# Moving two blocks of GpSimd sums at the start of a fused attention, MLP and adapter kernel

## The chip, the cores and the metric

One NeuronCore of a Trainium2 chip runs the whole program. The metric is the device time of one execution in microseconds (us), as the median of several runs. All data is float32. The engines are TensorE (PE; its weight loads are shown apart, as PEld), VectorE (DVE), ScalarE (ACT), GpSimd (POOL) and SyncE (SP). SP, ACT and POOL each also issue DMAs from their own queue; an engine works through its queue in order, and an instruction that waits holds up all behind it.

## The reference

Four sequences of 512 tokens of width 512 go through two layers. Shortened to what matters:

```python
# layer 0
q, k, v = x @ Wq, x @ Wk, x @ Wv
attn = softmax(q @ k.T * V ** -0.5)
attn_out = (attn @ v) @ Wp + bp
cms_out = gelu(attn_out @ cW1 + cb1) @ cW2 + cb2 + one_hot(target_codes)
concat = concatenate([attn_out, cms_out])
modifier = gelu(concat @ mW1 + mb1) @ mW2 + mb2
x = clip(x + cms_out + modifier, 0, 1)
# layer 1: one of three adapters for each sequence, chosen by stream
h = x + gelu(x @ W_down[stream] + b_down[stream]) @ W_up[stream] + b_up[stream]
out = layernorm(h) * ln_w[stream] + ln_b[stream]
```

## The kernel before

Every large product is made with seven block products in place of eight (Winograd's form of Strassen's scheme), in the MLP layers at two levels. A product of a left operand with blocks a11, a12, a21, a22 and a right operand with blocks b11, b12, b21, b22 needs four sums of the left blocks (s1 to s4) and four of the right (t1 to t4) besides the blocks themselves; the seven products are numbered 1 to 7, and product 5 takes s1 and t1, 6 takes s2 and t2, 7 takes s3 and t3, 3 takes s4, and 4 takes t4. `seven` runs them in a given order and combines them in PSUM with VectorE; when a block of the result is complete it calls `keep(half, columns, ps)`.

Two weights are folded ahead of their use: Wq with Wk to w_qk (cms0), and Wv with Wp to w_vp (cms1). `folded` does this with `small_product`, which takes the products in the order 1, 2, 5, 6, 7, 3, 4. The blocks of the result are complete after product 2 (half 0, columns 0), 7 (1, 1), 3 (0, 1) and 4 (1, 0), and `keep` copies each to w with ScalarE and has VectorE make the four sums of w, since w is next used as a left operand.

The four sequences go in two pairs. For each pair the loop in the kernel's body forms u = w_qk with x (`pair_product`, L638), then for each of the two sequences a softmax (`softmax`, whose matmuls are in `small_product` at L704), then the product of x's rows with the turned softmax (`small_product` again, left operand `left_operand(x_rows[s0 + k], s_x[k])`), and last w_vp with the two results. The sums of x's rows, s_x, are made by GpSimd in `left_sums`, which calls `weight_sums` (L198 to L201: s1, s2, s3, s4; s3 does not depend on s1). In pair 0 those of sequence 0 go to wslot2 and those of sequence 1 to wslot0, which before holds the sums of u that the first softmax uses. wslot2 also holds the sums of Wp that `right_sums` makes for the fold of w_vp (L741), so that the sums of sequence 0 are written, and made, behind that fold.

GpSimd also prepares the weights of the later layers. This is the generator `expansion`, of which `steps(expanding, n)` runs n parts. Its first part issues the loads of the raw cW1 blocks (`load_c1`, four DMAs, L235) and of x for sequences 2 and 3 (L142). `expand_c1` then has three parts for each of two units: four sums of 128x256 and a store from the upper half of slot1; eight sums of 128x512 into slot1, part and first, with the loads of the next raw blocks and two stores (c_outer, L258 and L259); and four sums of 128x256 with a store. Part and first are written again by the second unit, so that its sums wait for the stores of the first unit to land. Behind it come cW2 and mW1 (`expand`, L362 and L365).

x's first two sequences, Wv and Wp are loaded from SP's queue at the start, in this order, Wp into slot3; the sequences' rows stay in the tiles hidden.

The order of instructions within a queue is not that of the text. The framework under the kernel tracks the dependences of tiles and plans each engine's queue by its own costs: of the instructions that it takes for ready it places the one first that was written first. `keep_in_program_order` pins single instructions. So a move in the text shifts priorities, and the place in the queue is a result.

The part of the pair loop that the change touches reads before it:

```python
if pair == 0:
    s_v, t_wp = sums_in(slot[2]), sums_in(wslot[2])
    right_sums(wp, t_wp)
    then[7] = [lambda: transposed(chunks(wv), wv_t, left_from_psum(wv_t, s_v))]
pair_product(lhs_qk, begun, u, beside=beside_u(s_u, u), then=then)
if pair == 0:
    lhs_vp = folded(left_operand(wv_t, s_v), right_operand(wp, t_wp), w_vp, s_v)
steps(expanding, 6)
if pair == 0:
    left_sums(x_rows[s0], s_x[0])
```

Of the kernel before, what the change touches and what calls it, by code (L numbers as in the profile page):

```python
# [18 lines left out]
def kernel(  # L19
# [38 lines left out]
    nc = tc.nc  # L58
# [36 lines left out]
    slot = [wide[:, 4 * i : 4 * i + 4, :].rearrange("p c n -> p (c n)") for i in range(2)]  # L95
    slot += [const.tile([P, 2048], F32, name=f"slot{i}") for i in range(2, 8)]
    wslot = [const.tile([P, 2048], F32, name=f"wslot{i}") for i in range(4)]
# [16 lines left out]
    def weight(engines, src, dst):  # L114

        w = dst.rearrange("p (c n) -> p c n", c=4)
        n = 4 // len(engines)
        rows = src.rearrange("(h c p) n -> h p c n", c=n, p=P)
        for i, eng in enumerate(engines):
            eng.dma_start(out=w[:, n * i : n * (i + 1), :], in_=rows[i])  # L120
        return w
# [19 lines left out]
    def load_x(b, eng, dst):  # L141
        eng.dma_start(out=dst, in_=x[b].rearrange("(t p) v -> p t v", p=P))  # L142
        return dst
# [5 lines left out]
    x_rows = [load_x(b, nc.sync, x_places[b]) for b in range(2)]  # L149
    wv = weight((nc.sync, nc.sync), Wv, slot[2])  # L150
    wp = weight((nc.sync, nc.sync), Wp, slot[3])
# [44 lines left out]
    def weight_sums(a11, a12, a21, a22, s1, s2, s3, s4, eng=None):  # L196
        eng = eng or nc.gpsimd
        eng.tensor_tensor(s1, a21, a22, ALU.add)  # L198
        eng.tensor_tensor(s2, s1, a11, ALU.subtract)
        eng.tensor_tensor(s3, a11, a21, ALU.subtract)  # L200
        eng.tensor_tensor(s4, a12, s2, ALU.subtract)  # L201
# [13 lines left out]
    def flat(t):  # L215
        return t.rearrange("p c n -> p (c n)")
# [204 lines left out]
    def expansion():  # L421

        c2_units = [(cW2, False, c2_kept, u) for u in range(2)]
        load_c1(0)

        for b in range(2, B):
            x_rows.append(load_x(b, nc.gpsimd, x_places[b]))
        yield from expand_c1(0, lambda: load_c1(1))
        yield from expand_c1(1, lambda: load_raw(cW2, False, 0, slot[4:6]))

        constants()
        yield from expand_all(
            c2_units + m1_units, slot[4:6], (flat(part), slot[3], slot[1]), flat(first)
        )
# [39 lines left out]
    def steps(gen, n):  # L474
        for _ in range(n):
            next(gen, None)

    expanding = expansion()


    def transposed(get, dst, finish=None):

        begin_transposed(get, dst, finish)()
# [19 lines left out]
    def chunks(t):  # L503
        return lambda c: t[:, c, :]
# [6 lines left out]
    w_qk, w_vp = cms  # L511
# [35 lines left out]
    def add(dst, a, b):  # L547
        nc.vector.tensor_tensor(dst, a, b, ALU.add)  # L548
# [9 lines left out]
    def minus(out_, one, two):  # L558
        nc.vector.tensor_tensor(out_, one, two, ALU.subtract)
# [99 lines left out]
    def halves(t):  # L659

        return t[:, 0:2, :256], t[:, 2:4, :256], t[:, 0:2, 256:], t[:, 2:4, 256:]

    def left_operand(t, s):

        a11, a12, a21, a22 = halves(t)
        s1, s2, s3, s4 = (s[:, k] for k in range(4))
        return {1: a11, 2: a12, 3: s4, 4: a22, 5: s1, 6: s2, 7: s3}

    def left_sums(t, s):
        weight_sums(*halves(t), *(s[:, k] for k in range(4)))  # L670

    def right_operand(t, s):

        b11, b21, b12, b22 = halves(t)
        t1, t2, t3, t4 = (s[:, k] for k in range(4))
        return {1: b11, 2: b21, 3: b22, 4: t4, 5: t1, 6: t2, 7: t3}
# [41 lines left out]
    def sums_in(t):  # L718
        return t.rearrange("p (k c n) -> p k c n", k=4, c=2)
# [14 lines left out]

        return finish

    def right_sums(t, s):
        b11, b21, b12, b22 = halves(t)
        t1, t2, t3, t4 = (s[:, k] for k in range(4))
        for out_, one, two in ((t1, b12, b11), (t2, b22, t1), (t3, b22, b12), (t4, b21, t2)):  # L740
            nc.gpsimd.tensor_tensor(out_, one, two, ALU.subtract)  # L741

    def folded(lhs, rhs, w, s, then=None):


        s1, s2, s3, s4 = (s[:, k] for k in range(4))
        held = []

        def keep(half, columns, ps):
            dst = w[:, 2 * half : 2 * half + 2, 256 * columns : 256 * columns + 256]  # L750
            nc.scalar.copy(dst, ps)
            if (half, columns) == (1, 1):
                held.append(ps)
            elif (half, columns) == (0, 1):
                minus(s3, w[:, 0:2, :256], ps)
                minus(s2, held[0], s3)
                add(s1, held[0], w[:, 0:2, 256:])
            elif (half, columns) == (1, 0):
                minus(s4, ps, s2)

        small_product(lhs, rhs, keep, then, order=(1, 2, 5, 6, 7, 3, 4))
        return left_operand(w, s)
# [63 lines left out]
    lhs_vp = None  # L826
    next_operands = None

    def places(pair):

        return big[2 + 2 * pair : 4 + 2 * pair], (big[6:8], big[0:2])[pair]

    def first_operand(pair):
        xT, t_x = places(pair)
        return begin_transposed(
            chunks(x_rows[2 * pair]), xT[0], right_from_psum(xT[0], sums_in(flat(t_x[0])))
        )
# [68 lines left out]
    for pair in range(B // 2):  # L906
        s0, s1 = 2 * pair, 2 * pair + 1
        xT, t_x = places(pair)
        t_x = [sums_in(flat(t)) for t in t_x]
        u = big[4 - 2 * pair : 6 - 2 * pair]  # L910
        attn = big[6:8]
        s_u = [sums_in(wslot[k]) for k in range(2)]
        s_x = [sums_in(wslot[k]) for k in (2, 0)]
        t_p = t_x
        then = {}
        wv_t = mod[0]
        if pair:
            left_sums(x_rows[s0], s_x[0])
            s_x[1] = sums_in(flat(attn[1]))
            left_sums(x_rows[s1], s_x[1])  # L920
        if pair == 0:

            s_v, t_wp = sums_in(slot[2]), sums_in(wslot[2])
            right_sums(wp, t_wp)
            then[7] = [lambda: transposed(chunks(wv), wv_t, left_from_psum(wv_t, s_v))]
        pair_product(lhs_qk, begun, u, beside=beside_u(s_u, u), then=then)
        if pair == 0:

            lhs_vp = folded(left_operand(wv_t, s_v), right_operand(wp, t_wp), w_vp, s_v)
        steps(expanding, 6)  # L930
        if pair == 0:
            left_sums(x_rows[s0], s_x[0])
        pT, mix = u, xT

        def turn(k):
            transposed(lambda t: mod[k][:, t, :], pT[k], right_from_psum(pT[k], t_p[k]))

        for k in range(2):
            softmax(
                k, left_operand(u[k], s_u[k]), right_operand(xT[k], t_x[k]),  # L940
                {7: [lambda: turn(0)]} if k else None,
            )
            if k == 0 and pair == 0:
                left_sums(x_rows[s1], s_x[1])
        for k in range(2):
            if k == 0:
                def keep(half, tokens, ps):
                    nc.scalar.copy(
                        mix[0][:, 2 * half : 2 * half + 2, 256 * tokens : 256 * tokens + 256], ps
                    )  # L950
            else:
                operands, take = second_operand(*mix, mod)
                held = []

                def keep(half, tokens, ps):

                    if (half, tokens) == (1, 1):
                        held.append(ps)
                        return
                    take(half, (slice(0, 2), slice(256 * tokens, 256 * tokens + 256)), ps)  # L960
                    if (half, tokens) == (0, 1):
                        take(1, (slice(0, 2), slice(256, 512)), held[0])

            small_product(
                left_operand(x_rows[s0 + k], s_x[k]), right_operand(pT[k], t_p[k]), keep,
                {7: [lambda: turn(1)]} if k == 0 else None,
                nc.scalar.copy if k else nc.vector.tensor_copy,
            )
            steps(expanding, 6)
        then = {}  # L970
        if pair == 0:
            begun = {}
            then = {6: [lambda: first_operand(1)()], 4: [lambda: begun.update(both_operands(1))]}

        pair_product(lhs_vp, operands, attn, bp_c, then=then, at=pT[0] if pair else None)
        for k in range(2):
            nc.scalar.dma_start(out=attn_kept[s0 + k], in_=attn[k])
# [733 lines left out]
```

## Time and profile before

| what | us |
|---|---|
| median of three runs (lowest, highest) | 1183.7 (1181.69, 1184.09) |
| the profiled execution | 1187.64 |
| its span, first to last instruction | 1185.8 |
| PE busy in the span | 1163.2 |
| DVE busy | 884.6 |
| POOL busy | 579.1 |
| ACT busy | 297.9 |

The granted clock of TensorE was 0.998 in this execution. An execution's time is that of the span and of what lies around it. Each stretch of the timeline has a start, a duration, the engine, the line, the operation, what is written and read, and in brackets how long the engine was idle before and what released it. Names stand without their numbers, and names of tiles that share a helper's line tell its uses apart: `wslot<-hidden` on lines L198 to L201 is x's sums, `wslot<-slot` on L741 is Wp's.

How the engines were busy in the first 118 us (us of work and instructions in each stretch; the last columns are the granted clock, the DMA engines' busy share and GB/s):

```profile
0.00:10.65 10.65, 8.65 (x53) 7.90 (x54) 2.21 (x6) 4.21 (x7) 7.72 (x18) 1.00 0.81 232
10.65:29.28 18.63, 17.61 (x94) 14.26 (x93) 13.87 (x29) 7.98 (x15) 0.00 (x2) 1.00 1.01 375
29.28:55.10 25.82, 25.82 (x79) 13.21 (x78) 19.96 (x46) 8.02 (x15) 25.74 (x28) 1.00 0.60 200
55.10:62.40 7.30, 6.42 (x30) 5.35 (x30) 2.28 (x6) 0.58 (x1) 0.01 (x1) 1.00 0.79 303
62.40:75.65 13.25, 13.25 (x63) 11.67 (x62) 7.19 (x11) 2.24 (x4) 12.30 (x33) 1.00 0.20 81
75.65:99.98 24.33, 23.96 (x119) 20.57 (x118) 14.17 (x35) 15.25 (x48) 22.99 (x27) 1.00 0.61 193
99.98:109.85 9.87, 9.87 (x54) 8.51 (x52) 4.24 (x10) 5.69 (x11) 9.87 (x7) 1.00 0.14 60
109.85:118.00 8.15, 3.73 (x17) 2.97 (x17) 2.08 (x3) 0.58 (x1) 8.12 (x12) 1.00 0.26 104
```

The pairs of numbers are PE, PEld, DVE, ACT and POOL in this order. POOL does nothing between 10.65 and 29.28 and again between 55.1 and 62.4; PE has 3.73 us of work in the last 8.15.

### The profile page before, as it was taken

The page shows a single profiled execution, that of the slowest core. Times are in us where ns is not written, and L with a number is a line of the kernel's source. Part 1 is how long each engine was busy: PE and PEld are TensorE (multiplying, and loading weights), DVE is VectorE, ACT ScalarE, POOL GpSimd, SP SyncE. Part 2 cuts the span into 40 slices and gives each one's busy share as a digit, 9 for nine tenths or more (in the row PEclk, how much of TensorE's full clock was granted, in tenths as well). Part 3 has the DMA queues.
Part 4 walks back from the last instruction along what each step waited for, and adds up shares of the span by engine and source line. Part 5 has one row for each costly group of instructions (what it writes and reads, how often), then busy time and mean ns, then how long its engine had stood idle before and what let it go on. Part 6 is the DMA issues. An engine that isn't in the chain of part 4 may idle for free.

```text
span 1185.8 us, 13559 instructions
## 1 busy us (share of the span) xinstructions
PE 1163.2 (98%) x4937; PEld 916.0 (77%) x4937; DVE 884.6 (75%) x1192; ACT 297.9 (25%) x540; POOL 579.1 (49%) x634
## 2 busy tenths in 40 slices
PE   8998999999999999989999999999999999999996
PEld 7587548747468888878888887747888888888874
DVE  5744565477789967899699956669994588689954
ACT  4234334436520000012220027291000002230014
POOL 2889999998798048898400633530000001243002
PEclk9999999999999999999999999999999999999999
DMA  9634774897776588998856664262735454684601
GB/s 326 217 103 172 266 301 173 294 379 255 287 279 237 189 272 318 322 372 305 277 191 254 200 220 151 80 199 103 295 131 184 171 217 173 182 297 174 234 1 71
DMA packets 82609, 263.07 MB, mean 222 GB/s; under 512 B 8132, under 2 KB 37872, under 8 KB 67312
## 3 DMA queue, kind: packets, MB, share of 16 engines
q1 hardware_dynamic: 57184, 155.21, 36.5%
q0 software_dynamic: 23120, 97.57, 23.4%
q10 hardware_dynamic: 2240, 9.44, 2.0%
q8 instruction: 39, 0.64, 0.2%
q14 instruction: 26, 0.21, 0.1%
HBM read 190.88 MB, written 68.16 MB: 218 GB/s over the span
## 4 chain that ended last, share of the span: by engine, by line
PE 84%; DMA 7%; POOL 5%; issue 2%; DVE 2%; ACT 0%; ACTq 0%; POOLq 0%
PE i L1374 29%; PE i L1276 24%; PE c L1208 8%; PE sum L1133 7%; PE sum L638 6%; PE sum L704 4%; DMA wslot<-in_L_cond_mW 3%; PE up_ps L1499 2%; PE down_ps L1480 2%; DMA slot<-in_L_cond_Wp 2%; DMA c_outer<-part 1%; POOL wide L198 1%; PE up_ps L1494 1%; PE tr_ps L490 1%; DMA wide<-in_L_cond_Wk 1%
## 5 line engine op out<-in xcount | busy, mean ns | idle before, releaser
L1276 PE MATMUL i<-slot,wslot 128*128 128x256 f32 x1184 | 261.6, 379 | 1.6 <-DVE part L1003 1.4
L1276 PEld LDWEIGHTS i<-slot,wslot 128*128 128x128 f32 x1184 | 224.5, 190 | 33.5 <-issue 2.1
L1374 PE MATMUL i<-slot,wslot 128*128 128x256 f32 x896 | 202.5, 379 | 0.0
L1374 PEld LDWEIGHTS i<-slot,wslot 128*128 128x128 f32 x896 | 170.2, 190 | 23.1
L1010 ACT COPY first<-i 128x256 f32<-128x256 f32 (+1 forms) x56 | 26.8, 479 | 529.8 <-PE i L1374 259.2
L1374 PE MATMUL i<-hidden,wslot 128*128 128x256 f32 x576 | 132.2, 379 | 0.0
L1374 PEld LDWEIGHTS i<-hidden,wslot 128*128 128x128 f32 x576 | 109.4, 190 | 16.2 <-issue 1.4
L1003 DVE TENSOR_TENSOR part<-i,part 128x512 f32<-128x512 f32 (+1 forms) x156 | 90.8, 592 | 38.0 <-PE i L1276 27.3
L1032 ACT ACTIVATE hidden<-hidden,bias 128x512 f32<-128x512 f32 x128 | 84.4, 716 | 72.3 <-DVE hidden L548 62.4
L1597 POOL DMA_DIRECT2D slot<-xT_kept x4 | 2.9, 726 | 165.2 <-PE i L1276 165.2
L1208 PE MATMUL c<-slot,wslot 128*128 128x512 f32 x160 | 69.2, 592 | 0.0
L210 DVE TENSOR_TENSOR slot<-hidden 128x1024 f32<-128x1024 f32 x48 | 64.2, 1338 | 0.0
L1600 POOL TENSOR_TENSOR cms<-cms,slot 128x512 f32<-128x512 f32 x16 | 27.7, 1755 | 71.6 <-PE i L1276 38.5
L548 DVE TENSOR_TENSOR sum<-sum,wslot 128x512 f32<-128x512 f32 x48 | 33.4, 697 | 36.7 <-PE sum L704 24.7
L1208 PEld LDWEIGHTS c<-slot,wslot 128*128 128x128 f32 x160 | 30.4, 190 | 38.3 <-issue 35.4
L210 DVE TENSOR_TENSOR slot<-hidden,slot 128x1024 f32<-128x1024 f32 x48 | 59.3, 1235 | 0.3
L704 PE MATMUL sum<-hidden,wslot 128*128 128x256 f32 x232 | 53.8, 381 | 4.4 <-POOL wslot L200 2.7
L1003 DVE TENSOR_TENSOR part<-i,first 128x512 f32<-128x512 f32 (+1 forms) x62 | 36.4, 591 | 28.4 <-PE i L1276 17.6
L548 DVE TENSOR_TENSOR hidden<-part,hidden 128x2048 f32<-128x2048 f32 x20 | 53.2, 2658 | 0.5
L704 PEld LDWEIGHTS sum<-hidden,wslot 128*128 128x128 f32 x232 | 43.4, 190 | 11.3 <-POOL wslot L200 3.1
L1133 PE MATMUL sum<-mod,wslot 128*128 128x256 f32 x224 | 51.8, 379 | 0.0
L1133 PEld LDWEIGHTS sum<-mod,wslot 128*128 128x128 f32 x224 | 42.6, 190 | 5.8
(328 smaller groups left out, 2101.0 us busy)
## 6 DMA issues: line engine op xcount, KB each, us to landing
wslot<-m_kept SPq DMA_DIRECT2D x48, 1024.0 KB, 6.4
wslot<-m_kept SPq DMA_DIRECT2D x36, 512.0 KB, 4.9
wslot<-c_kept SPq DMA_DIRECT2D x16, 1024.0 KB, 7.0
slot<-in_L_cond_mW POOLq DMA_DIRECT2D x24, 512.0 KB, 7.0
wslot<-in_L_cond_mW SPq DMA_DIRECT2D x24, 512.0 KB, 6.4
wslot<-in_L_cond_cW SPq DMA_DIRECT2D x36, 256.0 KB, 5.3
slot<-in_L_cond_cW POOLq DMA_DIRECT2D x16, 512.0 KB, 7.7
m_kept<-wide POOLq DMA_DIRECT2D x6, 1024.0 KB, 8.6
```

Of the source, the lines that this page charges most:

```text
L210: i = eng.tensor_tensor(out_, one, two, ALU.subtract)
L548: nc.vector.tensor_tensor(dst, a, b, ALU.add)
L638: nc.tensor.matmul(ps, lhsT=lhs[p][:, c, r * P : (r + 1) * P], rhs=rhs[p][:, c, :], start=(first_ and c == 0), stop=(c == 1), skip_group_c ...
L704: nc.tensor.matmul(v[:, j, :], lhsT=lhs[p][:, c, j * P : (j + 1) * P], rhs=rhs[p][:, c, :], start=(first_ and j == 0 and c == 0), stop=(c ...
L1003: nc.vector.tensor_tensor(dst, ps, other, ALU.add)
L1010: nc.scalar.copy(c1, p1)
L1032: nc.scalar.activation(block[:, t, :], block[:, t, :], AF.Gelu, bias=bias_c[:, 8 * half + t : 8 * half + t + 1],)
L1133: nc.tensor.matmul(halves_of(ps)[:, j, :], lhsT=a[g][:, at_[q], j * P : (j + 1) * P], rhs=rhs[q][:, 0, :], start=(first_ and j == 0), stop ...
L1208: nc.tensor.matmul(ps, lhsT=lhs(c, t), rhs=operands[p][:, c, :], start=(c == 0), stop=(c == 1),)
L1276: nc.tensor.matmul(out_ps[:, j, :], lhsT=a[j][q][:, c, :], rhs=now[q][:, c, :], start=(c == 0), stop=(c == 1),)
L1374: nc.tensor.matmul(ps[:, :256], lhsT=a[k // 2][q][:, k % 2, :], rhs=now[q][:, k, :], start=(k == 0), stop=(k == 3),)
L1600: nc.gpsimd.tensor_tensor(cms[s][:, d, :], cms[s][:, d, :], in_rows[3][:, d, :], ALU.add)
```

## The change

In pair 0 the sums of Wp no longer go to wslot2 but into the four blocks of w_vp itself, each into one that the fold fills after its last reading: t1 lower right, t2 upper right, t3 upper left, t4 lower left. Since product 7 still reads t3, `folded` (for both folds) holds the block that is complete after product 2 in PSUM and copies it after product 7, ahead of the lower right one. With wslot2 free, the sums of x's rows of sequence 0 are written first, ahead of the expansion. The expansion's first two parts (the raw loads, the first four sums and a store, the eight sums and two stores) are written next, then the sums of Wp, and the remaining four parts behind the fold as before. In pair 1 nothing moves.

```diff
-    def right_sums(t, s):
+    def right_sums(t, w):
+
         b11, b21, b12, b22 = halves(t)
-        t1, t2, t3, t4 = (s[:, k] for k in range(4))
+        t3, t4, t2, t1 = halves(w)
         for out_, one, two in ((t1, b12, b11), (t2, b22, t1), (t3, b22, b12), (t4, b21, t2)):
             nc.gpsimd.tensor_tensor(out_, one, two, ALU.subtract)
+        return {1: b11, 2: b21, 3: b22, 4: t4, 5: t1, 6: t2, 7: t3}
...
         def keep(half, columns, ps):
-            dst = w[:, 2 * half : 2 * half + 2, 256 * columns : 256 * columns + 256]
-            nc.scalar.copy(dst, ps)
+            if (half, columns) == (0, 0):
+
+                held.append(ps)
+                return
+            if (half, columns) == (1, 1):
+                nc.scalar.copy(w[:, 0:2, :256], held.pop())
+            nc.scalar.copy(w[:, 2 * half : 2 * half + 2, 256 * columns : 256 * columns + 256], ps)
...
         wv_t = mod[0]
+        left_sums(x_rows[s0], s_x[0])
         if pair:
-            left_sums(x_rows[s0], s_x[0])
             s_x[1] = sums_in(flat(attn[1]))
             left_sums(x_rows[s1], s_x[1])
         if pair == 0:
 
-            s_v, t_wp = sums_in(slot[2]), sums_in(wslot[2])
-            right_sums(wp, t_wp)
+            steps(expanding, 2)
+            s_v = sums_in(slot[2])
+            rhs_wp = right_sums(wp, w_vp)
             then[7] = [lambda: transposed(chunks(wv), wv_t, left_from_psum(wv_t, s_v))]
         pair_product(lhs_qk, begun, u, beside=beside_u(s_u, u), then=then)
         if pair == 0:
 
-            lhs_vp = folded(left_operand(wv_t, s_v), right_operand(wp, t_wp), w_vp, s_v)
-        steps(expanding, 6)
-        if pair == 0:
-            left_sums(x_rows[s0], s_x[0])
+            lhs_vp = folded(left_operand(wv_t, s_v), rhs_wp, w_vp, s_v)
+        steps(expanding, 6 if pair else 4)
```

## The prediction

> **What bounds the kernel now.** I read first the page's busy shares, then the list of what TensorE waited for over the whole span.
>
> ```profile
> PE 1163.2 (98%) x4937; PEld 916.0 (77%) x4937; DVE 884.6 (75%) x1192; ACT 297.9 (25%) x540; POOL 579.1 (49%) x634
> ```
> ```profile
> PE sum L704 <- POOL wslot L200: 2.7, 1, 2.7
> PE i L1276 <- DMA wslot<-in_L_cond_mW: 2.5, 1, 2.5
> PE sum L704 <- POOL wslot L199: 1.7, 1, 1.7
> PE i L1276 <- DVE part L1003: 1.4, 1, 1.4
> PE idle_ps L193 <- DVE zeros L190: 1.1, 1, 1.1
> PE tr_ps L490 <- DMA hidden<-in_x: 1.0, 1, 1.0
> ```
>
> PE is busy 98% of the span, so a change that leaves its matmuls alone can give back only its waits. Just two of them, 2.7 and 1.7, are for GpSimd (POOL), both in small_product (L704). The timeline of PE shows where:
>
> ```profile
> 93.90 3.83 PE L704 MATMUL sum<-hidden,wslot 128*128 128x256 f32 x16
> ...
> 107.96 1.89 PE L704 MATMUL sum<-hidden,wslot 128*128 128x256 f32 x8
> 111.53 1.99 PE L704 MATMUL sum<-hidden,wslot 128*128 128x256 f32 x8 [1.69 <-POOL wslot L199]
> 113.37 1.89 PE L704 MATMUL sum<-hidden,hidden 128*128 128x256 f32 x8
> 117.99 3.72 PE L704 MATMUL sum<-hidden,wslot 128*128 128x256 f32 x16 [2.74 <-POOL wslot L200]
> ```
>
> This is the product of x's rows with the turned softmax, sequence 1 of pair 0. PE waits 1.69 for the second and 2.74 for the third sum of those rows: 4.43 together. Who makes POOL late is in its own timeline:
>
> ```profile
> 9.16 1.49 POOL L235 DMA_DIRECT2D slot<-in_L_cond_cW  x2 [1.51 <-DMA bias_rows<-in_L_cond_cb]
> 29.28 1.27 POOL L741 TENSOR_TENSOR wslot<-slot 128x512 f32<-128x512 f32 x1 [18.63 <-DMA slot<-in_L_cond_Wp]
> 30.50 0.77 POOL L142 DMA_DIRECT2D slot<-in_x  x1
> ...
> 35.74 0.74 POOL L198 TENSOR_TENSOR wide<-slot 128x256 f32<-128x256 f32 x1
> ...
> 62.42 1.27 POOL L200 TENSOR_TENSOR part<-slot 128x512 f32<-128x512 f32 x1 [7.31 <-DMA c_outer<-part]
> ...
> 92.51 1.26 POOL L198 TENSOR_TENSOR wslot<-hidden 128x512 f32<-128x512 f32 x1
> ...
> 99.98 2.37 POOL L362 TENSOR_TENSOR part<-slot,slot 128x1024 f32<-128x1024 f32 x1 [1.24 <-DMA c_outer<-part]
> ...
> 116.67 1.27 POOL L200 TENSOR_TENSOR wslot<-hidden 128x512 f32<-128x512 f32 x1
> ```
>
> POOL stands still for 18.63 until Wp lands, for 7.31 until a store of cW1's sums lands, and 1.24 for the next such store. In front of the second store's end it makes the sums of sequence 0 (from 92.51). Outside these waits it works without a gap, so what it loses up to 62 arrives at 117. The lines also show that the queue is not in the order of the text: a load of x (L142) stands between two sums of Wp, though it is written behind all four.
>
> **The change, part by part.** Two blocks of four POOL subtractions move; none is added or taken away.
>
> Wp's sums (four of 128x512 at about 1.27, 5.0 together) leave the head of the queue and come behind the second part of cW1's first expansion, where the wait of 7.31 now stands. They write the blocks of w_vp that the fold fills last, and wslot2 is free from the start. Sequence 0's sums (1.26 to 1.28 each, 5.0) take the place at the head, with x in place of Wp as what they wait for. The first rows of x are there at 17.44, when PE's transposes of them start after a wait of 1.0 for that load; Wp is there at 29.28. So the head of the queue is served by 17.4 + 5.0 = 22.4, against 35.0 (29.28 + four sums + two loads of x). The two x loads at 0.77 still have to be issued: 24.0.
>
> What then starts is cW1's expansion (35.74 now). It needs its raw blocks, four loads issued by POOL. If these stay ahead of the x sums, as they stand ahead of Wp's now (last issue 10.65), they land in a median of 9.7, by 20.4, and the expansion begins at 24.0: a lead of 11.7. If the queue puts all four behind the x sums, they go out by 22.4 + 3.0 = 25.4, and with the 8.4 that is the median landing of POOL's loads into these slots over the first 60 us they are there at 33.8: a lead of 1.9. With the longest of these, 11.2, it is 36.6, no lead but a loss of 0.9. The trace doesn't show which; I take the middle of 24.0 and 33.8, 28.9: a lead of **6.8**, bounds -0.9 and 11.7.
>
> [...]
>
> From there the lead is kept. The two parts with their loads and stores took 35.74 to 53.0, 17.3. The store of cW1's sums lands 10.4 after its issue; the wait of 7.31 for it now takes the 5.0 of Wp's sums, and the writes behind it come earlier by the whole lead. Behind the second expansion the same store comes again (issued 89.31, waited for until 99.98). Here sequence 0's sums used to fill the gap; taking them out buys **nothing**: POOL just waits some 6 instead of 1.24. Only the earlier start counts, not the 5.0 of work removed there.
>
> Sequence 1's sums come with the same lead, if they keep their place in the queue. They stand one by one among cW2's sums (105.3, 110.2, 116.7, 117.9) and use wslot0, which the four products of the first softmax free one after another; their place goes with those products, and what POOL has to do ahead of them is the same total in both kernels. So I take no shift of place; the bounds are in the rivals.
>
> PE needs a lead of 1.69 for the second sum and of 4.43 for the third (117.94 against 113.5). With 6.8 both waits go: **-4.43**. The group at 93.90 took 3.83 where its like take 3.62, its weight load having waited 0.2 for the first sum of sequence 0 (ended 93.77): **-0.2**.
>
> The fold's new order on ScalarE: the copy of the upper left block (0.58 in each of two folds) is made after the fifth instead of the second product. In the first fold ACT idles 5.50 ahead of 19.09, in the other 5.59 ahead of 63.10, and PE needs these blocks at 26.48 and 123.28: 0. Without that cover it is 0.6 each, 1.2. One PSUM bank is held longer; with its three companions in the fold and four of the transposes that is eight of eight, also 0, and within the same 1.2. Wp's sums must be ready for PE at 54.00; two parts after 28.9 is 46.2, the first sum 47.5, the last 51.2: 0, with 6.5 in hand. On the other side, if cW1's loads go behind x's, x lands with less traffic beside it, and PE's wait of 1.0 may shrink: 0 to -1.0; I take 0.
>
> Past 118 the chain of waits is PE nearly throughout; the next waits of size (1.37 and 2.52, between 505 and 531) come from VectorE and a weight load that follow PE's own progress. I let the gain through whole: **-4.6**. The profiled execution would go from 1187.6 (span 1185.8) to 1183.0; it was 3.9 above the median of the runs, so that on the median it is 1183.7 - 4.6 = **1179.1**, own range 1177.5 to 1180.3.
>
> **The rivals.**
>
> A. *A wait takes the place of the one removed.* cW1's loads land late, or Wp's sums stay ahead of the expansion, and the lead is about 2: of the third sum's 4.43 only that is gone. 1181.5. For it: the queue's own order, seen at 30.50. Against: with fewer loads beside them, Wp and cW1 would land sooner than at 29.28.
>
> B. *It does not do what it says.* The lead is nil, the gap ahead of 99.98 stays the store's, and the sums of sequence 1 come when they do now: 1183.7. For it: 1.24 of waiting at 99.98 with these sums in place says that the store is the limit there. Against: POOL would have to waste all of the 11.8 between 17.44 and 29.28.
>
> C. *Slower: sequence 1's sums fall behind cW2.* If POOL's place in the queue is further on when wslot0 comes free, more of cW2's first unit goes ahead of them. That unit runs from 99.98 to 126.9, less 5.1 for the x sums: 21.8. All of it ahead, with a lead of 2 to 6 (start 94 to 98): the third sum ends at 94 + 21.8 + 3.8 = 119.6 to 123.6, and PE waits 6 to 10 instead of 4.6: 1.5 to 5.5 lost, 1187.2 in the middle. It decides from where the added cW2 work exceeds the lead. For it: 5.3 of cW2 is already ahead of them. Against: the same total of work ahead.
>
> D. *Slower: Wp's sums too late.* PE's 54.00 gets later by each us that the expansion begins after 35.4 (54.0 - 1.3 - 17.3); from 40.0 on more is lost than won. That needs loads like Wv's (18.1 to land): 43.5, 8.1 lost less 4.6, 1187.2.
>
> **How the numbers follow.** Forecast 0.50, A 0.15, B 0.10, C 0.15, D 0.10. What a measurement here can tell from no change is about 0.2%, 2.4. Faster: the forecast and a third of A, 0.55; same: the rest of A and B, 0.20; slower: C and D, 0.25. The range runs from the forecast's lower end, 1177.5, to 1187.0, into C and D; some 0.1 lies above and little below.
>
> **What would show it.** PE without the 1.69 and 2.74 before L704's groups near 110 and 113; the first weight sum of cW1 on POOL near 29, and by 31.3 at the latest; Wp's sums between a c_outer store and the next write of part, ended before 54; a longer wait at the second c_outer store; sequence 1's third sum ended before 113.5. It is wrong if the expansion begins after 31.3, if cW2's first unit stands ahead of sequence 1's sums, if PE shows a new wait for cms in the fold at 54, or if the waits near 505 to 531 grow by what was won.

## The result, and the profile after

Over ten runs each, the changed kernel takes 1178.51 us in the median (1176.65 to 1180.32), the kernel before 1184.15 (1180.86 to 1185.49). The ratio is 0.9956, 95% interval 0.9944 to 0.9969: faster by 0.44%, which is 5.2 us (3.7 to 6.6). The forecast was 1179.1 and 4.6 less. The profiled execution took 1178.76 us, its span is 1176.8 and its mean granted clock 0.998.

What TensorE (PE) waited for in the whole span of the changed kernel (total, times, longest, in us):

```profile
PE i L1282 <- DVE part L1009: 1.4, 1, 1.4
PE idle_ps L193 <- DVE zeros L190: 1.1, 1, 1.1
PE sum L704 <- DVE sum L548: 0.8, 1, 0.8
PE sum L704 <- ACT wslot L613: 0.8, 2, 0.4
PE i L1282 <- DMA wslot<-in_L_cond_mW: 0.2, 1, 0.2
```

GpSimd (POOL) is gone from the list, and so are the waits for x's rows and for Wq. PE's timeline at the places that answer to those shown of before, with x's first transposes and the first product of the pair loop:

```profile
16.21 1.91 PE L490 MATMUL tr_ps<-ident,hidden 128*128 128x128 f32 x16
...
25.22 3.60 PE L638 MATMUL sum<-hidden,cms 128*128 128x512 f32 x8
...
92.58 3.62 PE L704 MATMUL sum<-hidden,wslot 128*128 128x256 f32 x16
...
106.42 3.62 PE L704 MATMUL sum<-hidden,wslot 128*128 128x256 f32 x16
109.87 1.89 PE L704 MATMUL sum<-hidden,hidden 128*128 128x256 f32 x8
111.60 3.62 PE L704 MATMUL sum<-hidden,wslot 128*128 128x256 f32 x16
```

Read against the lines of before: the first product comes 1.26 earlier (26.48), the group at 92.58 has lost its 0.2 (3.83 to 3.62), and the product that waited stands without a gap. Its last line is 6.39 earlier than before (117.99). POOL's timeline says how:

```profile
12.88 1.27 POOL L198 TENSOR_TENSOR wslot<-hidden 128x512 f32<-128x512 f32 x1 [7.15 <-DMA hidden<-in_x]
...
16.57 0.78 POOL L235 DMA_DIRECT2D slot<-in_L_cond_cW  x1
...
18.58 2.26 POOL L235 DMA_DIRECT2D slot<-in_L_cond_cW  x3
20.83 1.50 POOL L142 DMA_DIRECT2D slot<-in_x  x2
28.98 0.72 POOL L198 TENSOR_TENSOR wide<-slot 128x256 f32<-128x256 f32 x1 [6.65 <-PE sum L638]
...
46.26 2.51 POOL L742 TENSOR_TENSOR cms<-slot 128x512 f32<-128x512 f32 x2
...
55.38 1.27 POOL L200 TENSOR_TENSOR part<-slot 128x512 f32<-128x512 f32 x1 [1.41 <-DMA c_outer<-part]
...
90.18 2.35 POOL L362 TENSOR_TENSOR part<-slot,slot 128x1024 f32<-128x1024 f32 x1 [6.62 <-DMA c_outer<-part]
...
109.53 1.28 POOL L200 TENSOR_TENSOR wslot<-hidden 128x512 f32<-128x512 f32 x1
```

Sequence 0's sums run at 12.88, in the hole in which POOL waited for Wp. The loads of cW1 went behind them in the queue, the first (16.57) ahead of the last sum (17.36). cW1's sums begin at 28.98 in place of 35.74. The line names PE's product at L638 as what ended that wait, but the instruction waits for several semaphores, and in wp_only and loads_first (below) the same sum begins at 18.64 and 23.54, before PE's first product at L638. By the kernel's text the sum reads the third of the four loads, issued near 19.3; it is the candidate left, though this trace has no landing time for it. Wp's sums stand behind the stores, at 46.26, and leave 1.41 of the wait of 7.31. The next wait for such a store has grown from 1.24 to 6.62. Sequence 1's third sum ends at 110.81; PE takes it at 111.60.

### The profile page after: what moved, and what is told of

It is laid out like the page before. It is cut to its first block, busy times and chain, and to the rows that moved or that the text cites. A ratio compares the mean times of both kernels' runs of the same rounds, so it can differ in the third digit from the quotient of the medians.

```text
span 1176.8 us, 13556 instructions
## 1 busy us (share of the span) xinstructions
PE 1163.0 (99%) x4937; PEld 918.0 (78%) x4937; DVE 880.6 (75%) x1192; ACT 297.4 (25%) x540; POOL 578.2 (49%) x634
## 4 chain that ended last, share of the span: by engine, by line
PE 95%; DVE 2%; DMA 1%; ACT 1%; issue 0%
PE i L1380 29%; PE i L1282 26%; PE sum L704 9%; PE sum L638 8%; PE c L1214 8%; PE sum L1139 7%; PE up_ps L1505 2%; PE down_ps L1486 2%; PE tr_ps L490 1%; DMA wslot<-in_L_cond_mW 1%; PE up_ps L1500 1%; DVE hidden L548 1%; DVE slot L210 1%; PE tr_ps L869 0%; PE idle_ps L193 0%
## 5 line engine op out<-in xcount | busy, mean ns | idle before, releaser
L1009 DVE TENSOR_TENSOR part<-i,first 128x512 f32<-128x512 f32 (+1 forms) x62 | 36.4, 591 | 28.6 <-PE i L1282 17.4
```

The source lines that it names most:

```text
L1009: nc.vector.tensor_tensor(dst, ps, other, ALU.add)
```

## The experiments

Each row gives the median, the ratio to the kernel before as it ran in the same batch, and from one profile the start of the first product at L638, PE's waits for POOL, the start of cW1's sums and the end of sequence 1's third sum (for x1_twice of its second making).

| kernel | us | ratio (95% interval) | first L638 | waits for POOL | cW1's sums | third sum |
|---|---|---|---|---|---|---|
| before | 1184.15 | | 26.48 | 4.4 | 35.74 | 117.94 |
| changed | 1178.51 | 0.9956 (0.9944 to 0.9969) | 25.22 | 0 | 28.98 | 110.81 |
| ctl_before | 1184.46 (one run) | | 26.16 | 4.0 | 35.60 | 116.95 |
| ctl_after | 1178.32 | 0.9947 (0.9923 to 0.9970) | 25.24 | 0 | 28.55 | 109.89 |
| x_only | 1178.03 | 0.9939 (0.9917 to 0.9961) | 25.18 | 0 | 28.92 | 110.04 |
| wp_only | 1180.79 | 0.9964 (0.9947 to 0.9980) | 26.93 | 0 | 18.64 | 110.84 |
| loads_first | 1180.32 | 0.9957 (0.9939 to 0.9975) | 26.17 | 0 | 23.54 | 105.51 |
| blocks_only | 1186.59 | 1.0021 (1.0006 to 1.0036) | 25.49 | 4.9 | 35.74 | 118.99 |
| fold_only | 1185.21 | 0.9999 (0.9985 to 1.0014) | 26.25 | 3.6 | 35.15 | 116.71 |
| x_twice | 1179.43 | 0.9944 (0.9922 to 0.9965) | 25.19 | 0 | 28.73 | 111.69 |
| x1_twice | 1189.58 | 1.0044 (1.0024 to 1.0064) | 25.17 | 6.0 | 28.65 | 112.99 |

**Both kernels once more.** ctl_before and ctl_after are the two kernels as they are.

> The changed kernel once more. Both theories: no PE wait for POOL before 118 and the first product L638 near 25.2, time 5 to 6 us under before. The wait for mW1's raw block near 525 (2.5 us in the profile of before, 0.2 in that of the changed kernel) may be anything from 0 to 3 if it is a matter of the execution; if it belongs to the change, it is 0.2 again.

> The kernel before once more, for its profile. PE's waits for POOL are 1.7 and 2.7 to within 0.3, the first product L638 at 26.5 to within 0.3. If the wait for mW1's raw block near 530 is a matter of the execution, it will differ from 2.5 by more than 0.5.

The starts and the waits for POOL came again: 25.24 and none, 26.16 and 1.2 with 2.7. The 1.2 is half a microsecond less than 1.7 and outside what was expected, as the first c_outer store landed 1.1 earlier here; the first product was 0.3 earlier. ctl_after is 6.5 under before, a little more than expected. The wait for mW1's block was 1.4 in one and absent in the other, where the first profiles had 0.2 and 2.5: it belongs to the execution, not to the change. Of the 9.0 us between the two first spans, 2.3 are therefore chance.

**One half at a time.** x_only leaves Wp's sums written ahead of the expansion:

```diff
         if pair == 0:
 
-            steps(expanding, 2)
             s_v = sums_in(slot[2])
             rhs_wp = right_sums(wp, w_vp)
...
-        steps(expanding, 6 if pair else 4)
+        steps(expanding, 6)
```

> Only sequence 0's sums are moved to the head; Wp's sums (in w_vp's blocks) come next, ahead of cW1's expansion, which has its last raw load behind them. My theory: cW1's sums start when Wp is in and summed, 29 to 33, a lead of 3 to 7 over 35.7; the store wait of 7 us comes back in full; the lead at the third sum of sequence 1 is 2 to 6, and PE waits 0 to 2 us for POOL there. PE's start is that of the changed kernel (first product L638 near 25.2). Time 3.5 to 6 us under before. Rival (it is Wp's sums under the store that buy it): PE waits 3 to 5 us, time 1 us under before.

wp_only puts sequence 0's sums back behind the fold:

```diff
-        left_sums(x_rows[s0], s_x[0])
         if pair:
+            left_sums(x_rows[s0], s_x[0])
...
         steps(expanding, 6 if pair else 4)
+        if pair == 0:
+            left_sums(x_rows[s0], s_x[0])
```

> Only Wp's sums are moved behind cW1's second part; sequence 0's sums stand behind the fold again. My theory (what counts is how early cW1's expansion starts; the sums' own 5 us don't count): cW1's loads are issued by 10.7 and land near 20, so its sums start at 21 to 23 in place of 35.7, and PE waits for neither of sequence 1's sums: 4.4 us of PE waiting gone. PE's start goes back to that of before (x's rows land at about 17.4, a wait of some 1 us, first product L638 at 26.5). Time 4 to 5 us under before, 1 us over the changed kernel. Rival (the gain comes from taking sequence 0's sums out of the queue ahead of sequence 1's): PE still waits 3 to 5 us for POOL, time within 1 us of before.

Either half alone takes away both waits for POOL, which both rivals had excluded. x_only is 6.8 under before, more than the 3.5 to 6 expected. POOL in x_only:

```profile
20.84 2.62 POOL L742 TENSOR_TENSOR cms<-slot 128x512 f32<-128x512 f32 x2 [0.33 <-DMA slot<-in_L_cond_Wp]
...
28.92 0.73 POOL L198 TENSOR_TENSOR wide<-slot 128x256 f32<-128x256 f32 x1 [0.75 <-PE sum L638]
...
54.49 1.27 POOL L200 TENSOR_TENSOR part<-slot 128x512 f32<-128x512 f32 x1 [6.16 <-DMA c_outer<-part]
```

Wp is there at 20.84, not at 29.28, and POOL waits 0.33 for it: with cW1's loads held back behind sequence 0's sums, there is less beside it to land (argued from the two traces; no run changes this alone). Wp's sums then fit into the wait for cW1, whose sums begin at 28.92 as in the changed kernel. So the store's wait (6.16 here) comes back and costs nothing, and the runs show no gain from Wp's place under the store beside the other half: 1178.03 against 1178.32 for ctl_after in the same batch.

POOL in wp_only:

```profile
18.64 0.72 POOL L198 TENSOR_TENSOR wide<-slot 128x256 f32<-128x256 f32 x1 [6.85 <-issue]
...
41.23 1.26 POOL L742 TENSOR_TENSOR cms<-slot 128x512 f32<-128x512 f32 x1 [5.28 <-DMA slot<-in_L_cond_Wp]
```

Here the loads of cW1 and of two sequences of x go out by 11.8, and cW1's sums begin at 18.64, a lead of 17 and earlier than the 21 to 23 expected. Much of it is lost again: POOL waits for Wp until 41.23, most likely for all that was put beside it (argued from the traces as well), and sequence 0's sums, which were placed at 54.69 by the plan, push the small constants in among cW2's sums. The third sum of sequence 1 is 7.1 earlier than before. That is enough for PE, but PE's start is late: it waits 0.87 and 0.64 for x's rows, first product at 26.93. The time, 2.5 us over ctl_after where 1 was expected, has that in it (1.7).

**The start.** loads_first issues cW1's four loads ahead of sequence 0's sums:

```diff
     def expansion():
 
         c2_units = [(cW2, False, c2_kept, u) for u in range(2)]
-        load_c1(0)
...
+        if pair == 0:
+            load_c1(0)
         left_sums(x_rows[s0], s_x[0])
```

> The changed kernel with cW1's four raw loads issued ahead of sequence 0's sums. My theory (the 1.3 us won at the very start come from those loads being held back, so that Wq's quarters and x land with less traffic): x's rows land near 17.4 again, PE waits about 1 us for them and shorter for Wq, first product L638 at 26.3 to 26.7; cW1's sums start at about 24; no PE wait for POOL; time 1 to 1.5 us over the changed kernel. Rival (the start differs from run to run, or by the plan of the other engines): first product at 25.2, time as the changed kernel.

PE's timeline of loads_first, then POOL's:

```profile
17.13 1.94 PE L489 MATMUL tr_ps<-ident,hidden 128*128 128x128 f32 x16 [1.01 <-DMA hidden<-in_x]
...
26.17 3.60 PE L637 MATMUL sum<-hidden,cms 128*128 128x512 f32 x8
```
```profile
17.07 1.27 POOL L198 TENSOR_TENSOR wslot<-hidden 128x512 f32<-128x512 f32 x1 [6.87 <-DMA hidden<-in_x]
```

x's rows land at 17.07 and not at 12.88, PE waits 1.01 for them again, and the first product comes 0.95 later than in the changed kernel, a little less than expected. The median is 2.0 over ctl_after, more than expected, but the intervals of the two ratios overlap, so that the profile and not the median carries this. Holding the loads back won most of the time at the start: in the five profiles with the loads behind these sums POOL has x's rows at 12.9 to 13.4 and PE never waits for them; in five of the six with the loads ahead PE waits 0.8 to 1.1 ahead of their first transposes and starts these at 17.1 to 17.4. In the sixth, blocks_only, it does not wait, and its first product stands at 25.49: so up to 1 us of this can come without holding the loads back, by chance or by that kernel's plan, which the runs don't tell apart. The waits for Wq are no part of it. ctl_before has none with the loads ahead, and x1_twice has two (0.7 together) with the loads held back and its first product at 25.17. That cW1's sums began 5.4 earlier here (23.54), and the third sum ended 5.3 earlier, bought nothing: PE had no wait left to lose.

**Where the sums lie.** blocks_only moves no sums in the text; Wp's go to w_vp's blocks, which leaves wslot2 free:

```diff
-        left_sums(x_rows[s0], s_x[0])
         if pair:
+            left_sums(x_rows[s0], s_x[0])
...
-            steps(expanding, 2)
             s_v = sums_in(slot[2])
...
-        steps(expanding, 6 if pair else 4)
+        steps(expanding, 6)
+        if pair == 0:
+            left_sums(x_rows[s0], s_x[0])
```

> Neither block of sums is moved in the text; only the place of Wp's sums is w_vp's blocks and the fold's order the new one, so that wslot2 is free from the start. Wp's sums wait at the head as in the kernel before. My theory (an early start of cW1's expansion is what counts, the rest is permutation): that start is 35 to 36 as before; with wslot2 free sequence 0's sums come some 30 us earlier in the queue, into the place of the small constants near 66, and the constants go among cW2's sums; the lead that the second store gives is eaten by these, the third sum of sequence 1 ends at 117 to 121, and PE waits 4 to 7 us for POOL. Time from 0 to 3 us over before. Rival (freeing wslot2 alone is the gain): PE waits under 1 us for POOL, time 4 us under before.

What PE waited for in POOL, and POOL's timeline, in blocks_only:

```profile
PE sum L704 <- POOL wslot L198: 2.7, 1, 2.7
PE sum L704 <- POOL wslot L200: 2.2, 1, 2.2
```
```profile
35.74 0.75 POOL L198 TENSOR_TENSOR wide<-slot 128x256 f32<-128x256 f32 x1
...
64.73 1.29 POOL L198 TENSOR_TENSOR wslot<-hidden 128x512 f32<-128x512 f32 x1
...
94.61 2.36 POOL L362 TENSOR_TENSOR part<-slot,slot 128x1024 f32<-128x1024 f32 x1 [5.56 <-issue]
...
103.98 0.29 POOL L545 TENSOR_SCALAR idx_u<-pos,ex_bn 128x2 int32<-128x2 f32 x1
...
117.72 1.27 POOL L200 TENSOR_TENSOR wslot<-hidden 128x512 f32<-128x512 f32 x1
```

As expected, and the one kernel of the halves that is slower than before (by 2.5 us, 0.7 to 4.3): sequence 0's sums move up to 64.73 on their own, the small constants that stood there go among cW2's sums (the index at 103.98), and the lead of 5.4 that POOL has at cW2's first sum is eaten by them. With the start at 35.74, sums moved out from in front of sequence 1's don't help. It is a case like rival C of the prediction, with a cause of its own.

blocks_only and wp_only differ only in where the expansion's first two parts are written: ahead of Wp's sums in wp_only, behind them here. Sequence 0's sums move up and the constants fall among cW2's sums in both. cW1's sums begin at 18.64 in the one and at 35.74 in the other, where Wp's sums stand ahead of them in POOL's queue and wait 19.13 for Wp; sequence 1's third sum ends at 110.84 and 118.99, and PE, whose own start is 1.4 apart, waits 0 and 4.9 for POOL. This is the cleanest evidence that the early start takes the waits away.

The waits themselves are only 0.5 longer than before and PE's first product is 1.0 earlier, so they don't make blocks_only slower. PE's groups behind the two waits do:

```profile
109.64 5.51 PE L704 MATMUL sum<-hidden,wslot 128*128 128x256 f32 x16 [2.73 <-POOL wslot L198]
...
119.05 5.41 PE L704 MATMUL sum<-hidden,wslot 128*128 128x256 f32 x16 [2.18 <-POOL wslot L200]
```

Without a wait ahead of it such a group takes 3.62. The two took 3.7 more together, with a mean granted clock of 0.73 from 109.60 to 115.00 and of 0.68 from 119.00 to 124.30; the last section comes back to this.

fold_only is the kernel before with the changed `keep` in `folded` and nothing else.

> The kernel before with nothing but the fold's new order: the upper left block is held in PSUM and copied after product 7. My theory: ScalarE's idle time takes the copy and a PSUM bank is free, so nothing moves: PE's first product L638 at 26.5, waits of 1.7 and 2.7 for POOL as before, time within 1 us of before. Rival (the later copy or the held bank is a cost that the changed kernel hides): PE waits 0.6 to 1.2 us longer before 118, time 1 us over before.

The ratio is 0.9999 (0.9985 to 1.0014), the first product stands at 26.25, and PE waits 0.9 and 2.7 for POOL, the first less than expected: the runs show no cost of the held bank and the late copy.

**The dose.** x_twice and x1_twice make POOL's work longer; both only repeat sums that are already there.

```diff
         steps(expanding, 6 if pair else 4)
+        if pair == 0:
+            left_sums(x_rows[s0], s_x[0])
```

> The changed kernel with sequence 0's sums made a second time behind the fold (the same values into the same place): 5 us more on POOL ahead of sequence 1's sums. My theory (the third sum has only some 0.8 us in hand): where these sums fall into one of POOL's waits they are free, where not they come through; between 0 and 5 us of PE waiting for POOL, and whatever delay the third sum has beyond 0.8 against the changed kernel (110.8 there) is PE's wait to within 0.3. Rival (sequence 1's sums are no longer what PE waits for, some other wait follows): the third sum's delay beyond 0.8 does not appear as a PE wait.

The repeated sums went into the place of the small constants, which again went among cW2's sums; the third sum ended at 111.69, 0.88 later than in the changed kernel, and PE's group that takes it began at 111.75 in place of 111.60. That is the edge, as told; it tells little about more.

```diff
             if k == 0 and pair == 0:
                 left_sums(x_rows[s1], s_x[1])
+                left_sums(x_rows[s1], s_x[1])
```

> The changed kernel with sequence 1's sums made twice, the same values into the same place, so that PE has to wait for the second making. My theory (PE follows these sums to the us once they are later than it): the second making of the second sum is ended some 5 us behind the first making of the third (110.8 in the changed kernel), near 116; PE needs it at 108.2 and waits 7 to 8 us; the first product L638 behind it moves from 116.8 to 124 or 125, and the time is 7 to 8 us over the changed kernel. Rival (such a wait is taken back by slack further on): PE waits as long, but the time is less than 4 us over the changed kernel.

PE's timeline of x1_twice, then the stretches around the wait (us of work of PE, PEld, DVE, ACT, POOL; granted clock, DMA share, GB/s):

```profile
106.37 1.89 PE L704 MATMUL sum<-hidden,wslot 128*128 128x256 f32 x8
114.27 3.78 PE L704 MATMUL sum<-hidden,wslot 128*128 128x256 f32 x8 [6.01 <-POOL wslot L199]
117.84 3.07 PE L704 MATMUL sum<-hidden,hidden 128*128 128x256 f32 x8
120.75 3.62 PE L704 MATMUL sum<-hidden,wslot 128*128 128x256 f32 x16
```
```profile
106.00:114.20 8.20, 2.26 (x11) 1.65 (x9) 0.69 (x1) 0.98 (x2) 8.18 (x11) 0.95 0.16 64
114.20:117.80 3.60, 3.54 (x8) 2.86 (x9) 0.00 (x0) 0.00 (x0) 3.58 (x5) 0.50 0.17 71
117.80:120.70 2.90, 2.90 (x9) 2.36 (x8) 0.70 (x1) 0.00 (x0) 2.90 (x4) 0.58 0.40 120
```

PE waits 6.0, less than the 7 to 8 expected, since the second making of the second sum was placed earlier than I took it to be (ended at 114.21). The next product at L638 is nevertheless 9.1 later than in the changed kernel (125.92), more than expected, and the time 11 over it (1189.58). So nothing of the wait is taken back by slack further on; on the contrary something was added. The two groups behind the wait took 3.78 and 3.07 in place of 1.89 each, 3.1 more together, with the granted clock at 0.50 and 0.58. The 6.0 and the 3.1 make the 9.1. The spans of the two profiles are 9.9 apart; the 11 is between medians of two batches, and its last part I can't place.

## Why the prediction was right

**The two waits, -4.43.** Right. Between the first x sums' product and the next L638, PE is 6.50 earlier at its end and 1.54 earlier at 106.42, so that this stage gave 4.96: the two waits and some 0.5 of restarts behind them. In these traces a group without a wait starts some 0.17 before the one ahead of it has ended (109.87 against 106.42 and 3.62), and a group behind a wait took 0.1 longer (1.99 and 3.72 against 1.89 and 3.62). Either half of the change gives it.

**The lead at cW1's sums, 6.8 between -0.9 and 11.7.** It measured 6.76, but by another sum, and that it met the middle of two bounds was luck. The loads went behind sequence 0's sums, the late case. The prediction had that case at 33.8, a lead of 1.9, because it took 17.4 for x's landing from a trace in which cW1's loads share the traffic; this step was wrong by 4.5. Held back, the loads let x land at 12.9, and POOL's head was served by 22.3. If the third load ended the wait, it landed some 9.6 after its issue near 19.3, as the prediction's median of 9.7 had it. Counted as the prediction did, from the last load's issue (20.84), the wait ended 8.1 later, 7.5 in ctl_after, under the 8.4 that the prediction took. The 35.0 given for the head of before has one load of x in it, not two; nothing hangs on it.

**The gap at the second store.** Right: POOL waits 6.62 there, "some 6". That taking 5 us of sums out of this gap buys nothing agrees with blocks_only, where the gap grew to 5.56 and PE's waits stayed.

**Sequence 1's sums keep their place.** They did not, and "the lead is kept" was wrong twice, in ways that nearly cancel. The lead had grown to 9.8 at cW2's first sum: a load of b_down no longer stood in front (1.3), a sum of cW1 was made within an earlier wait (0.7), and the second store landed sooner after its issue (0.8). It had shrunk to 7.1 at the third x sum, since a sum and a store of cW1 (1.3) and two sums of cW2 (1.4) came in ahead of that. That 7.1 lies near the 6.8 of the sum is luck. I also forgot that PE itself gets earlier, by its start and by the restarts, so that the lead needed is 6.3 (117.94 to 111.60) and not 4.4. This left 0.8 in hand (110.81 to 111.60), where the sum had 2.4.

**Wp's sums in time for PE, 0.** Right: the last ended at 51.9, and PE's first product that reads them came at 52.74 for the first of them, made by 47.5.

**The start, taken as 0 with a bound of -1.0.** The term that was mis-sized: it measured -1.26, beyond its bound. 1.19 of it lies between the start of the group ahead of x's transposes and theirs (12.80 to 17.44 before, 12.76 to 16.21 after): the wait of 1.02 and some 0.2 of restart behind it, which the bound left out. The mechanism was the one named, less traffic beside x; loads_first gives 0.95 of it back, and blocks_only shows that a part can come without it.

**The fold, 0 with 1.2 as a bound.** fold_only shows none, to within its interval.

**What comes behind.** The waits of 1.37 and 2.52 near 505 to 531 were taken as passing the gain on. The first came again (1.39); the second varies from one execution to the next between 0 and 2.5 and is in neither kernel's account.

With 1.26, 0.2 and 4.96 the stage up to 123 gave 6.5 in the two first profiles. In the second pair, ctl_before and ctl_after, it gave 5.5, and the medians are 5.6 apart. So the forecast of 4.6 had the waits right and was short by the start and the restarts.

## What to carry to other kernels

When an engine is late for a product, ask when its chain starts and through which waits that lateness reaches the product. Work taken out of a gap that a store sets was worth nothing here; an early start, of 7 us by one way and 17 by the other, took both waits away. A load issued at the very start was not free here, though nothing waited for it yet: 2 MB held back by 10 us let x land 4.2 earlier (12.88 against 17.07 in loads_first), and gave about 1 of the 5 to 6 us won; Wp was there 8.4 earlier in x_only (20.84 against 29.28). And where a framework plans the queues, freeing a buffer moves work by itself (blocks_only): look at the queue's new order before crediting the line that was moved.

## What the runs showed of the hardware

A wait of PE can cost more than its length. In fold_only the second wait for POOL was as long as before, 2.73, but the group behind it took 5.41, where the same group took 3.72 in the kernel before. The group in fold_only and the stretch of its first 3.2 us, and the same group in the kernel before:

```profile
116.76 5.41 PE L704 MATMUL sum<-hidden,wslot 128*128 128x256 f32 x16 [2.73 <-POOL wslot L200]
```
```profile
116.76:120.00 3.24, 3.24 (x8) 2.60 (x9) 0.00 (x0) 0.00 (x0) 3.24 (x5) 0.56 0.16 63
```
```profile
117.90:121.60 3.70, 3.61 (x17) 3.20 (x18) 0.70 (x1) 0.58 (x1) 3.70 (x6) 1.00 0.16 63
```

The granted clock is 0.56 in the one and 1.00 in the other, after the same wait. At the lower clock most matmuls of 128x256 took 0.634 in x1_twice and blocks_only, in place of 0.379 each in the kernel before. Of the 59 executions of the kernel before beside the experiments, 22 have a mean clock under 0.997, and their median is 1185.7 against 1183.9 of the others. Of 53 executions of the kernels without a wait for POOL (changed, ctl_after, x_only, wp_only, loads_first, x_twice) none has; of those that wait most, blocks_only and x1_twice, 17 of 19 have. So the change also took away a slowdown that hits the kernel before in some executions, about 1.8 each time. That the waits are its cause rests on these counts and on the order of events in the profiles, not on a run that holds the clock.

The length of a wait alone does not tell whether the clock falls. Behind the 2.74 in the kernel before, the group took 3.72, and behind 2.75 in ctl_before as well; behind 2.73 in fold_only it took 5.41, and in blocks_only the groups behind 2.73 and 2.18 took 5.51 and 5.41. What decides it these runs don't show.
